# Cross-attention block on one core: VectorE's transposes ahead of a block's second work item, and statistics and norms in other places

## The chip, the cores and the metric

The kernel runs on one core of a Trainium2 chip. The metric is device time in microseconds (us), median of the runs; lower is better. Everything is computed in fp32.

## The reference

A transformer block with cross-attention, for B = 4 batches of L = 512 tokens, D = 512, H = 16 heads of HD = 32, and an inner size of 2048. The mask of the drawn inputs is all ones.

```python
x = layer_norm(hidden_states, ln1_w, ln1_b)                      # (4, 512, 512)
q = (x @ q_w + q_b)                 # -> (B, H, L, HD)
k = (encoder_hidden_states @ k_w + k_b)
v = (encoder_hidden_states @ v_w + v_b)
scores = einsum('bhqd,bhkd->bhqk', q, k) * scale
scores = where(mask, scores, finfo.min)
out = einsum('bhqk,bhkd->bhqd', softmax(scores), v)
hidden = out @ cproj_w + cproj_b + hidden_states
y = layer_norm(hidden, ln2_w, ln2_b)
y = gelu(y @ fc_w + fc_b, approximate=True) @ proj_w + proj_b
return hidden + y
```

## The kernel before

**Tiles.** There are 128 partitions, so a batch has 4 token tiles (NT), and the 16 heads make 4 groups of 4 heads (NG, HG). A window `w` (0 to 15) is one batch with one group of heads. A window has two halves, and a *block* `p` (0 to 31, `w, half = divmod(p, 2)`) is the attention of one half: two query tiles `q0`, `q1`, four heads each, 512 keys.

**A block** (function `block`) does this. `scores` issues eight matmuls (L259), each into a PSUM bank of its own. All dense accumulators, `tp`, `av` and score tiles take PSUM banks in one rotation of eight (`acc_tile`): the n-th tile can be written only when the reader of tile n-8 is done with it. `soften` takes one score tile: VectorE adds the mask `mb` and reduces a minimum (L265), ScalarE takes the exponential with its sum (L269). The results stand in six slots. `turn` transposes a pair of slots in 32x32 squares on VectorE (L277), four times per block, into `tb`. The sums' reciprocal (VectorE, L294) is spread by ScalarE (`rr`, L296) and transposed by VectorE too (L300). `exchange` then calls `copies`, which moves the 32-partition strips of `tb` to their places: four copies on POOL (L329) and twelve DMAs, most of them on SP's queue (L335), into `pT`, `gt` or `xe`, as soon as that target is free. Two blocks later (three in the first blocks) `attend` multiplies with `v` on TensorE (`av`, L352), and VectorE scales `av` into `oT` (L357), which also frees the target and calls `exchange` again.

**Work inside blocks.** Three calls `fill(0)`, `fill(1)`, `fill(2)` in `block` take the other work from a list per block, made with `put(p, ...)`: projections `prep_k`, `prep_q`, `prep_v` (TensorE; ScalarE copies `acck`, `accq`, `accv` out at L219, L230, L244; POOL adds the bias of `v` at L251 or, for window 0, in `v_bias`), the first layer norm of the next batch, the output projection `cproj`, and the MLP's products. `run` takes items until their costs reach a budget: an item has a cost (CHAIN for a dense chain, more for an FC product, 0 for what `do` makes), and an item is still taken if the spent cost and half of its own stay within the budget.

**Layer norm.** `ln_stat` is statistics and aggregate of one token tile on VectorE (L127, L128), `ln_rs` a short chain on POOL (L133 to L140), `ln_norm` normalises one tile on ScalarE (L145) for the keys in `NORM_ACT`, on VectorE (L149) for the others, `ln_turn` transposes on TensorE (`tp`, L158) and applies weight and bias while copying out, on VectorE (L161) or ScalarE (L163). A key is (1 or 2, batch): first or second norm.

**Products of the MLP.** An FC item runs a product on TensorE (L507), ScalarE copies one part `p` out (L510), VectorE adds up (L467), ScalarE takes the gelu (L525). The gelu and the exponential need different tables, which ScalarE loads when they alternate. A projection item (PJ) accumulates `accp` on TensorE (L555), and VectorE adds it to the hidden state (L559).

**Order.** `manual_schedule` means that each engine gets its instructions in the order in which the program writes them. So the order of calls in `block`, the lists given to `put` and the code ahead of the loop fix every engine's queue; the waits between engines come on top. TensorE runs the next block's scores while VectorE and ScalarE finish the block before.

**The start.** Ahead of the loop, the loads go to SP's queue in the order of the program: weights, context and `x` of batch 0, `row`, mask, weights of window 1, then the eight `fc_w` tiles of `load_mlp` (L456). `x` of batch 1 is loaded into the `xn` tiles after that (`load_x`, L176). Its statistics are taken in the fills of blocks 0 and 1, and its four norms, on ScalarE, in block 2.

Of the kernel before, what the change touches and what calls it, by code (L numbers as in the profile page):

```python
# [12 lines left out]
F32 = mybir.dt.float32  # L13
# [7 lines left out]
P = 128  # L21
B, L, D, H = 4, 512, 512, 16
HD = D // H
INNER = 4 * D
NT = L // P
# [7 lines left out]
NW = B * NG  # L33
# [6 lines left out]
NORM_ACT = BY_ACT + ((2, 0), (2, 1))  # L40
# [10 lines left out]
def xattn_block(ctx: ExitStack, tc: tile.TileContext, x, encT, mask, q_w, k_w, v_w, c_w, fc_w, p_w, vecs, rows, out):  # L51
    nc = tc.nc
# [5 lines left out]
    const, keep, hids, tiles, small = pools(ctx, const=1, keep=1, hids=6, tiles=4, small=4)  # L58
# [17 lines left out]
    gt = const.tile([P, NI * (PW + 2 * HD)], F32, tag="gt", name="gt")  # L76
# [36 lines left out]
    S = {}  # L113
# [9 lines left out]
    def ln_stat(key, t, src):  # L123
        if t == 0:
            S["mv", key] = small.tile([P, NT, 2], F32, tag="mv", name=f"mv{key[0]}_{key[1]}")
        st = small.tile([P, 6], F32, tag="st", name=f"st{key[0]}_{key[1]}_{t}")
        nc.vector.bn_stats(st, src)  # L127
        nc.vector.bn_aggr(S["mv", key][:, t, :], st)  # L128
# [12 lines left out]
            S["nm", key] = nm  # L141

    def ln_norm(key, t, dst, src):
        if key in NORM_ACT:
            nc.scalar.activation(  # L145
                dst, src, AF.Identity, bias=S["nm", key][:, t : t + 1], scale=S["rs", key][:, t : t + 1]
            )
            return
        nc.vector.tensor_scalar(  # L149
            dst, src, S["mv", key][:, t, 0:1], S["rs", key][:, t : t + 1], ALU.subtract, ALU.mult  # L150
        )
# [17 lines left out]
    def load_enc(b):  # L169
        for d in range(ND):  # L170
            queue(b).dma_start(out=eT[:, d, :], in_=encT[b, ts(d, P), :])
# [30 lines left out]
    def load_w(w, queue=None, names=("wk", "wq", "wv")):  # L202

        if w >= NW:
            return
        g = w % NG
        for i, (n, src) in enumerate((("wk", k_w), ("wq", q_w), ("wv", v_w))):
            if n in names:
                S[n, w] = kqv_w(w, i)
                (queue or Q[0]).dma_start(out=S[n, w], in_=src[:, g, :, :])  # L210
# [11 lines left out]
    def prep_q(w):  # L222
        b, g = divmod(w, NG)
        qT = k_q(w, 1)
        acc = acc_tile(f"accq_{w}")
        for d in range(ND):
            nc.tensor.matmul(acc, S["wq", w][:, d, :], xT[:, d, :], start=(d == 0), stop=(d == ND - 1))  # L227
        load_w(w + 2, names=("wq",))

        nc.scalar.activation(qT, acc, AF.Identity, bias=qb[:, g : g + 1], scale=-scale)  # L230
        S["qT", w] = qT

    def prep_v(w):
        b = w // NG
        v = five.tile([P, NT, P], F32, tag="v", name=f"v_{w}")
        acc = acc_tile(f"accv_{w}")
        for t in range(NT):
            for d in range(ND):
                nc.tensor.matmul(  # L239
                    acc[:, ts(t, P)], eT[:, d, ts(t, P)], S["wv", w][:, d, :],  # L240
                    start=(d == 0), stop=(d == ND - 1),
                )
        load_w(w + 2, names=("wv",))
        nc.scalar.copy(v, acc.rearrange("p (t f) -> p t f", t=NT))  # L244
        S["v", w] = v
        if w:
            v_bias(w)

    def v_bias(w):
        v, bias = S["v", w], row[:, 2, ts(w % NG, P)]  # L250
        nc.gpsimd.tensor_tensor(v, v, bias[:, None, :].broadcast_to([P, NT, P]), ALU.add)  # L251
# [9 lines left out]
    def soften(w, qt, *heads):  # L261
        for h in heads:
            s = score_tile()
            mn = small.tile([P, 1], F32, tag="mn", bufs=2 * HG, name=f"mn_{w}_{qt}_{h}")
            nc.vector.tensor_tensor_reduce(  # L265
                out=s, in0=S["sc", w, qt][h], in1=S["mb", w // NG], scale=1.0, scalar=FMAX,
                op0=ALU.add, op1=ALU.min, accum_out=mn,
            )
            nc.scalar.activation(s, s, AF.Exp, bias=mn, scale=-1.0, accum_out=S["sums", w][:, qt, h : h + 1])  # L269
            if h % 2:  # L270
                S["ps", w, qt, h // 2] = score_pair()

    def turn(w, qt, k):

        tb = S["tb", w, qt // 2]
        tv = tb[:, :, :PW].rearrange("p j (a t h q) -> p a h t j q", a=2, t=NT, h=HG)
        nc.vector.transpose(tv[:, qt % 2, 2 * k : 2 * k + 2], S["ps", w, qt, k])  # L277

    def block(w, half, fill):

        q0, q1 = 2 * half, 2 * half + 1
        if half == 0:
            S["sums", w] = small.tile([P, NT, HG], F32, tag="sums", name=f"sums_{w}")
        tb = S["tb", w, half] = two.tile([P, NI, PW + 2 * HD], F32, tag="tb", name=f"tb_{w}_{half}")
        scores(w, q0)
        scores(w, q1)
        soften(w, q0, 0, 1, 2, 3)
        soften(w, q1, 0, 1)
        turn(w, q0, 0)
        soften(w, q1, 2, 3)  # L290
        fill(0)
        turn(w, q0, 1)
        rs = small.tile([P, 2, HG], F32, tag="rsum", name=f"rsum_{w}_{half}")
        nc.vector.reciprocal(rs, S["sums", w][:, 2 * half : 2 * half + 2, :])  # L294
        rr = one.tile([P, 2, HG, HD], F32, tag="rr", name=f"rr_{w}_{half}")
        nc.scalar.copy(rr, rs[:, :, :, None].broadcast_to([P, 2, HG, HD]))  # L296
        turn(w, q1, 0)
        fill(1)
        turn(w, q1, 1)
        nc.vector.transpose(  # L300
            tb[:, :, PW:].rearrange("p j (a q) -> p a j q", a=2), rr.rearrange("p a h d -> p (a h d)")
        )
        waiting.append((w, half))
        if w < NW - 1 or half == 0:
            exchange()
        fill(2)

    waiting, held = [], {}
# [5 lines left out]
    def exchange():  # L314

        while waiting and target(*waiting[0]) not in held:
            w, half = waiting.pop(0)
            held[target(w, half)] = w, half
            copies(w, half)
# [513 lines left out]
    CHAIN, TURN = 3.4, 0.5  # L833

    def do(fn):
        return [(0.0, fn)]
# [13 lines left out]
    def turns1(b):  # L850
        return [(TURN, lambda d=d: ln1_turn(b, d)) for d in range(ND)]
# [10 lines left out]
    def inputs(b):  # L862
        ln = [(0.0, lambda part=part: ln1(b, part)) for part in range(3)]
        return do(lambda: load_x(b)), ln, turns1(b), do(lambda: load_enc(b))

    def run(work, budget=None):

        spent = 0.0
        while work and (budget is None or spent + work[0][0] / 2 <= budget):
            cost, fn = work.pop(0)  # L870
            fn()
            spent += cost
        return spent
# [15 lines left out]
    nc.sync.dma_start(out=row, in_=rows[None, :, :].broadcast_to([P, 3, D]))  # L889
    load_mask(0, nc.sync)  # L890
    load_w(1, nc.sync, ("wv", "wq"))

    load_mlp()

# [3 lines left out]
    prep_v(0)  # L898
    prep_k(1)
    run(turns1(0))  # L900
    x1, x2, x3, x4 = inputs(1)
    run(x1)
    load_h(0, *range(NT))
    nc.sync.dma_start(out=wc, in_=c_w)
    make_mb(0)
    nc.vector.tensor_scalar(qb, vec[:, QB : QB + NG], 0.0, -scale, ALU.add, ALU.mult)
    prep_q(0)
    v_bias(0)


    mlp = []
# [3 lines left out]
    def some(n):  # L915
        taken = []
        while n > 0:
            n -= 1 if mlp[0][0] == CHAIN else 2
            taken.append(mlp.pop(0))
        assert n == 0  # L920
        return taken
# [4 lines left out]
    def h_(b, *ts_):  # L926
        return do(lambda: load_h(b, *ts_))
# [7 lines left out]
    def rs(b):  # L935
        return do(lambda: ln_rs((2, b)))

    def stat(b, *ts_):
        return do(lambda: [stat2(b, t) for t in ts_])
# [6 lines left out]
    def put(p, *work, before=()):  # L946

        work = [item for part in work for item in part]
        ahead[p] = list(before)
        fills[p] = work  # L950

    k2, q2, v2 = A(2)
    k3, q3, v3 = A(3)
    k4, q4, v4 = A(4)
    k5, q5, v5 = A(5)
    k6, q6, v6 = A(6)
    put(0, [(CHAIN, lambda: prep_v(1)), v2, k2], x2[:1])
    put(1, [k3, (0.0, lambda: prep_q(1)), (CHAIN, lambda: (prep_v(3), load_enc(1)))], x2[1:2])
    put(2, [q2], x2[2:], [k4])
    put(3, [q3, v4])  # L960
    put(4, x3[:2], [k5], x3[2:])
    put(5, [v5, q4])
# [15 lines left out]
    k, q, v = A(10)  # L978
    put(13, [k], some(2), [v], x2[:1])
    put(14, [q], some(2))  # L980
    put(15, some(2), x2[1:2], some(2))

    k, q, v = A(11)
    put(16, h_(1, 0, 1), x2[2:], [k, q], x3[:2], some(2), x3[2:3])
    put(17, [v], x3[3:], h_(1, 2, 3), x4, cb(1), C(1))
    k, q, v = A(12)
    put(18, [q], some(2), [k])
    put(19, some(2), [v])
    k, q, v = A(13)
    put(20, [k, q], some(2), stat(1, 0, 1))  # L990
    put(21, [v], some(2), stat(1, 2, 3), rs(1))
    k, q, v = A(14)
    t2 = turns2(1)
    put(22, [k, q], norm(1, 0, 1), some(2), norm(1, 2, 3))
# [14 lines left out]
    for p in range(2 * NW):  # L1009
        w, half = divmod(p, 2)  # L1010
        if half == 0 and w and w % NG == 0:
            make_mb(w // NG)
        run(ahead[p])
        for pair in due.get(p, ()):
            attend(*divmod(pair, 2))

        def fill(n, work=fills[p]):
            run(work, CHAIN if n < 2 else None)

        block(w, half, fill)  # L1020
    exchange()

    first_c = FIRST * FQ // 2
    load_h(B - 1, *range(NT))
# [59 lines left out]
```

## Time and profile before

| | before |
| --- | --- |
| median of 3 runs | 777.32 us (776.58 to 777.48) |
| the profiled execution | 776.39 us, of which the span is 774.6 us |
| PE (TensorE matmul) busy | 767.5 us, 99% of the span, 4442 matmuls |
| DVE (VectorE) busy | 622.6 us, 80% |
| ACT (ScalarE) busy | 338.4 us, 44% |
| POOL (GpSimd) busy | 298.7 us, 39% |
| DMA | 119.37 MB, mean 154 GB/s |
| chain that ended last | PE 96%, DVE 2%, DMA 1% |

In the rows, a time stands at the start of a line if it is one of the timeline (us from the start of the span, then duration, engine, line, operation, tiles written and read, and how many instructions of a kind lie together). What stands in brackets is the idle time ahead of the instruction and what ended it. Matmuls are pipelined: a matmul that stands in the queue behind a waiting one, or waits behind a running one, is shown as busy.

### The profile page before, as it was taken

Reading aid. Unit: us, or ns where it says so; the run is one execution under the profiler, and the core shown is the slowest. Engines: PE = TensorE matmul, PEld = TensorE weight load, DVE = VectorE, ACT = ScalarE, POOL = GpSimd, SP = SyncE. Lnnn points to the kernel's source line nnn. Section 1 sums busy time; section 2 is a strip of 40 time slices with the busy share of each in tenths; the row PEclk is TensorE's granted clock in tenths of the full one; section 3 lists DMA queues with packets and bytes.
Section 4 is the critical chain, followed back from the end, with each engine's and each line's share of the span. In section 5 each row is a group of like instructions: output and inputs, shape, how many; then the busy total and the mean of one; then the engine's idle time right before and its main releaser. Section 6 shows DMA issues by size and latency. Waiting matters only on the chain.

```text
span 774.6 us, 12975 instructions
## 1 busy us (share of the span) xinstructions
PE 767.5 (99%) x4442; PEld 519.3 (67%) x4442; DVE 622.6 (80%) x1262; ACT 338.4 (44%) x760; POOL 298.7 (39%) x311
## 2 busy tenths in 40 slices
PE   9999999999999999999999999999999999999998
PEld 6655555467754745565554556446888889988897
DVE  3798999787988857877887889877878999679863
ACT  2577767477774626547663567401201221012200
POOL 1435446377355364224573553350060024300052
PEclk9999999999999999999999999999999999999999
DMA  8978778457766766664656586783523330023001
GB/s 329 309 223 216 183 200 229 125 151 177 224 167 162 183 181 169 156 173 121 162 136 189 144 240 167 207 254 122 199 84 98 90 115 14 28 83 95 1 16 41
DMA packets 54818, 119.37 MB, mean 154 GB/s; under 512 B 10417, under 2 KB 13617, under 8 KB 54625
## 3 DMA queue, kind: packets, MB, share of 16 engines
q1 hardware_dynamic: 53424, 114.88, 53.3%
q0 software_dynamic: 896, 2.82, 1.2%
q10 hardware_dynamic: 432, 0.86, 0.5%
q8 instruction: 35, 0.57, 0.3%
q14 instruction: 31, 0.25, 0.1%
HBM read 58.22 MB, written 6.82 MB: 84 GB/s over the span
## 4 chain that ended last, share of the span: by engine, by line
PE 96%; DVE 2%; DMA 1%; SPq 0%; issue 0%; ACT 0%; ACTq 0%; POOL 0%; DVEq 0%; POOLq 0%
PE q L507 25%; PE accp L555 9%; PE sc L259 8%; PE accv L239 8%; PE acck L217 7%; PE r L645 7%; PE accq L227 7%; PE av L352 7%; PE accc L392 7%; PE q4p L682 2%; PE q1p L700 2%; PE tp L158 2%; PE q2p L682 1%; DMA xe<-tb 1%; DVE tb L277 1%; PE warm L888 1%
## 5 line engine op out<-in xcount | busy, mean ns | idle before, releaser
L269 ACT ACTIVATE ptt<-ptt,mn 128x512 f32<-128x512 f32 x256 | 181.6, 710 | 125.8 <-DVE mn L265 125.8
L265 DVE CUSTOM_DVE_ANT_0 ptt<-sc,mb 128x512 f32<-128x512 f32 x256 | 161.5, 687 | 21.5 <-PE sc L259 16.9
L277 DVE STREAM_TRANSPOSE tb<-ptt 128x1024 f32<-128x1024 f32 x128 | 155.1, 1221 | 0.0
L329 POOL COPY pT<-tb 32x1088 f32<-32x1088 f32 x96 | 104.3, 1087 | 52.8 <-DVE oT L357 32.8
L555 PE MATMUL accp<-pbt,gt 128*128 128x512 f32 x192 | 85.1, 597 | 0.0
L507 PE MATMUL q<-yT,gt 128*128 128x256 f32 x320 | 78.9, 379 | 0.0
L259 PE MATMUL sc<-pbt 32*128 32x512 f32 x512 | 70.7, 616 | 1.5 <-ACT pbt L230 0.8
L555 PEld LDWEIGHTS accp<-pbt,gt 128*128 128x128 f32 x192 | 35.7, 190 | 47.6 <-issue 39.7
L507 PEld LDWEIGHTS q<-yT,gt 128*128 128x128 f32 x320 | 60.8, 190 | 8.7 <-issue 0.5
L525 ACT ACTIVATE ga<-ga,vec 128x512 f32<-128x512 f32 x40 | 26.7, 714 | 87.9 <-DVE ga L467 87.9
L239 PEld LDWEIGHTS accv<-ptt,xe 128*128 128x128 f32 x512 | 59.0, 192 | 8.4 <-DVE mn L265 5.3
L507 PE MATMUL q<-ys,gt 128*128 128x256 f32 x240 | 61.7, 379 | 0.0
L239 PE MATMUL accv<-ptt,xe 128*128 128x128 f32 x512 | 60.2, 276 | 0.0
L217 PE MATMUL acck<-xe,ptt 128*128 128x512 f32 x128 | 58.7, 601 | 0.0
L227 PE MATMUL accq<-xe,ptt 128*128 128x512 f32 x128 | 58.2, 597 | 0.0
L392 PE MATMUL accc<-wc,oT 128*128 128x512 f32 x128 | 56.1, 595 | 0.0
L507 PEld LDWEIGHTS q<-ys,gt 128*128 128x128 f32 x240 | 45.5, 190 | 6.6 <-DVE gt L464 0.4
L259 PEld LDWEIGHTS sc<-pbt 32*128 32x128 f32 x512 | 28.5, 183 | 30.9 <-issue 17.0
L269 ACT ACTIVATION_READ_ACCUMULATOR ptt<-ptt,mn 128x1 f32 x256 | 47.8, 187 | 0.0
L352 PE MATMUL av<-pT,v 128*32 128x256 f32 x768 | 46.4, 382 | 0.0
L217 PEld LDWEIGHTS acck<-xe,ptt 128*128 128x128 f32 x128 | 23.5, 192 | 31.0 <-issue 22.5
L251 POOL TENSOR_TENSOR v<-v,row 128x512 f32<-128x512 f32 x16 | 20.3, 1272 | 61.5 <-ACT v L244 61.5
(179 smaller groups left out, 1187.1 us busy)
## 6 DMA issues: line engine op xcount, KB each, us to landing
pT<-tb SPq DMA_DIRECT2D x288, 136.0 KB, 2.4
pbt<-p_w_dram SPq DMA_DIRECT2D x40, 256.0 KB, 3.1
gt<-fc_w_dram SPq DMA_DIRECT2D x40, 256.0 KB, 2.6
gt<-tb SPq DMA_DIRECT2D x48, 136.0 KB, 2.8
pbt<-fc_w_dram SPq DMA_DIRECT2D x24, 256.0 KB, 3.3
xe<-tb SPq DMA_DIRECT2D x42, 136.0 KB, 2.8
ptt<-k_w_dram SPq DMA_DIRECT2D x16, 256.0 KB, 3.9
xe<-encT_dram SPq DMA_DIRECT2D x16, 256.0 KB, 4.0
```

The costliest lines, as they stand in the source:

```text
L217: nc.tensor.matmul(acc, S["wk", w][:, d, :], eT[:, d, :], start=(d == 0), stop=(d == ND - 1))
L227: nc.tensor.matmul(acc, S["wq", w][:, d, :], xT[:, d, :], start=(d == 0), stop=(d == ND - 1))
L239: nc.tensor.matmul(acc[:, ts(t, P)], eT[:, d, ts(t, P)], S["wv", w][:, d, :], start=(d == 0), stop=(d == ND - 1),)
L259: nc.tensor.matmul(S["sc", w, qt][h], qT[r, ts(qt, P)], kT[r, :], start=True, stop=True)
L265: nc.vector.tensor_tensor_reduce(out=s, in0=S["sc", w, qt][h], in1=S["mb", w // NG], scale=1.0, scalar=FMAX, op0=ALU.add, op1=ALU.min, acc ...
L269: nc.scalar.activation(s, s, AF.Exp, bias=mn, scale=-1.0, accum_out=S["sums", w][:, qt, h : h + 1])
L277: nc.vector.transpose(tv[:, qt % 2, 2 * k : 2 * k + 2], S["ps", w, qt, k])
L329: nc.gpsimd.tensor_copy(pT[ts(i, HD), i], tb[ts(i, HD), i])
L352: nc.tensor.matmul(av[ts(h, HD), : 2 * P].rearrange(shape, **kw), v[:, t, ts(h, HD)], p[t][h], start=(t == 0), stop=(t == NT - 1),)
L392: nc.tensor.matmul(acc, S["oT", b][:, g, ts(t, P)], wc[:, g, :], start=(g == 0), stop=(g == NG - 1))
L507: nc.tensor.matmul(o, x[:, k], y[:, k], start=(k == 0), stop=(k == 1))
L555: nc.tensor.matmul(acc, gT[q % 2][:, k, ts(t, P)], S["pw", b, q * FQ + k], start=(k == 0), stop=(k == FQ - 1))
```

## The change

The change has six parts.

1. In `block`, VectorE's second `turn` of `q0` goes ahead of `fill(0)`, and the last `turn` and the transpose of `rr` go ahead of `fill(1)`; the reciprocal now stands behind the first `turn` of `q1`. `exchange` stays behind `fill(1)`. In the last block it is now called there as well, and no longer behind the loop.
2. `fill(0)` does nothing where the block's first item costs more than CHAIN. Of the lists given, that is block 29, which starts with an FC product: it now has its two products in `fill(1)` and `fill(2)`.
3. `x` of batch 1 is loaded into `gt` ahead of `load_mlp`, its statistics and `ln_rs` stand ahead of the first `prep_q`, and its four norms (`norm1`, ScalarE, from `gt` into the `xn` tiles) in the last fill of block 0.
4. The last two of the key (2, 0)'s four norms (block 10) go from ScalarE to VectorE.
5. The four norms of batch 3 (VectorE) go from block 16 into block 15, between the last two PJ items.
6. The four statistics of key (2, 1) and its `ln_rs`, which stood at the end of blocks 20 and 21, go into block 20 ahead of its PJ items.

TensorE's instructions keep their order, one for one.

```diff
     def ln_norm(key, t, dst, src):
-        if key in NORM_ACT:
+        if key in NORM_ACT and (key != (2, 0) or t < 2):
...
         soften(w, q1, 0, 1)
         turn(w, q0, 0)
         soften(w, q1, 2, 3)
+        turn(w, q0, 1)
         fill(0)
-        turn(w, q0, 1)
+        turn(w, q1, 0)
         rs = small.tile([P, 2, HG], F32, tag="rsum", name=f"rsum_{w}_{half}")
         nc.vector.reciprocal(rs, S["sums", w][:, 2 * half : 2 * half + 2, :])
         rr = one.tile([P, 2, HG, HD], F32, tag="rr", name=f"rr_{w}_{half}")
         nc.scalar.copy(rr, rs[:, :, :, None].broadcast_to([P, 2, HG, HD]))
-        turn(w, q1, 0)
-        fill(1)
         turn(w, q1, 1)
         nc.vector.transpose(
             tb[:, :, PW:].rearrange("p j (a q) -> p a j q", a=2), rr.rearrange("p a h d -> p (a h d)")
         )
         waiting.append((w, half))
-        if w < NW - 1 or half == 0:
-            exchange()
+        fill(1)
+        exchange()
         fill(2)
...
     load_w(1, nc.sync, ("wv", "wq"))
+    for t in range(NT):
+        nc.sync.dma_start(out=gt[:, ts(t, D)], in_=x[1, ts(t, P), :])
     load_mlp()
...
     run(turns1(0))
-    x1, x2, x3, x4 = inputs(1)
-    run(x1)
     load_h(0, *range(NT))
     nc.sync.dma_start(out=wc, in_=c_w)
     make_mb(0)
     nc.vector.tensor_scalar(qb, vec[:, QB : QB + NG], 0.0, -scale, ALU.add, ALU.mult)
+    for t in range(NT):
+        ln_stat((1, 1), t, gt[:, ts(t, D)])
+    ln_rs((1, 1))
     prep_q(0)
     v_bias(0)
+
+    def norm1(b, *ts_):
+        for t in ts_:
+            S["xn", b][t] = tiles.tile([P, D], F32, tag="xn", name=f"xn1_{b}_{t}")
+            ln_norm((1, b), t, S["xn", b][t], gt[:, ts(t, D)])
+
+    S["xn", 1] = [None] * NT
+    x3 = turns1(1)
...
-    put(0, [(CHAIN, lambda: prep_v(1)), v2, k2], x2[:1])
-    put(1, [k3, (0.0, lambda: prep_q(1)), (CHAIN, lambda: (prep_v(3), load_enc(1)))], x2[1:2])
-    put(2, [q2], x2[2:], [k4])
+    put(0, [(CHAIN, lambda: prep_v(1)), v2, k2], do(lambda: norm1(1, *range(NT))))
+    put(1, [k3, (0.0, lambda: prep_q(1)), (CHAIN, lambda: (prep_v(3), load_enc(1)))])
+    put(2, [q2], [k4])
...
-    put(15, some(2), x2[1:2], some(2))
+    put(15, some(2), x2[1:2], some(1), x2[2:], some(1))
...
-    put(16, h_(1, 0, 1), x2[2:], [k, q], x3[:2], some(2), x3[2:3])
+    put(16, h_(1, 0, 1), [k, q], x3[:2], some(2), x3[2:3])
...
-    put(20, [k, q], some(2), stat(1, 0, 1))
-    put(21, [v], some(2), stat(1, 2, 3), rs(1))
+    put(20, [k, q], stat(1, 0, 1, 2, 3), rs(1), some(2))
+    put(21, [v], some(2))
...
         def fill(n, work=fills[p]):
-            run(work, CHAIN if n < 2 else None)
+            if n or not work or work[0][0] <= CHAIN:
+                run(work, CHAIN if n < 2 else None)
 
         block(w, half, fill)
-    exchange()
```

## The prediction

> **What bounds the kernel now.** I read the page first, then PE's waits, then the chain that ended last in order of time, and last the timelines around each place where the chain runs slow.
>
> ```profile
> PE 767.5 (99%) x4442; PEld 519.3 (67%) x4442; DVE 622.6 (80%) x1262; ACT 338.4 (44%) x760; POOL 298.7 (39%) x311
> ```
>
> ```profile
> PE av L352 <- DMA xe<-tb: 0.9, 1, 0.9
> ```
>
> TensorE is busy throughout and carries the chain, and the order of instructions shows that the change leaves its stream as it is, matmul for matmul. So the time moves only by what TensorE waits. Its own waits look tiny (the longest but the start's is 0.9 us, above), but a matmul that waits behind a running one counts as busy. The eight score tiles of a block are the same work each time, so their group shows the hidden waits:
>
> ```profile
> 47.38 1.93 PE sc L259 x16
> ...
> 58.24 3.19 PE sc L259 x16
> ...
> 80.00 3.62 PE sc L259 x16
> ```
>
> 1.93 us is the undisturbed group. Block 3 (58.24) pays 1.26 on top, block 5 (80.00) 1.69; blocks 21 and 22 follow below. The last score tiles of a group need PSUM banks that the block before used last: its dense accumulators and `av`. What frees them late is a VectorE or ScalarE queue that runs late. These places, and the 0.9 us before the last `attend`, are all that can be won.
>
> **Statistics and norms of batch 1.** In block 2 ScalarE runs four norms ahead of the `rr` copy:
>
> ```profile
> 55.99 2.32 DVE L277 STREAM_TRANSPOSE tb<-ptt 128x1024 f32<-128x1024 f32 x2
> 56.26 2.92 ACT L145 ACTIVATE xn<-xn,nm,rs 128x512 f32<-128x512 f32 x4
> 59.08 0.39 ACT L296 COPY rr<-rsum 128x256 f32<-128x256 f32 x1
> 59.50 0.45 DVE L300 STREAM_TRANSPOSE tb<-rr 128x256 f32<-128x256 f32 x1 [1.19 <-ACT rr L296]
> ```
>
> The norms hold `rr` to 59.08, so VectorE stands still for 1.19 us, and the `acck` copy behind `rr` and the `oT` product behind the `rr` transpose free their banks only after 59.9, inside block 3's group. The change moves the norms to block 0. Then, with the reciprocal now behind one more transpose (2.32 for two, 1.16 each), `rr` runs at 57.2, `acck` leaves at 58.2, the `rr` transpose at 58.3, `oT` at 58.9. The second half of the group is due at 58.17 + 0.97 = 59.1: nothing is late next. **Gain 1.26.** In block 0 the four norms (2.92) stand behind the last `acck` copy, and block 1's exponentials queue behind them by about 1.7 us. VectorE's four statistics leave blocks 0 and 1 (3.2 us), which pays for that: I get the end of VectorE's block 1 at 46.4, before the next scores at 47.4.
>
> The statistics go to the start, ahead of the first softmax:
>
> ```profile
> 10.61 5.88 SPq L456 DMA_DIRECT2D pbt<-fc_w_dram  x8
> 23.20 0.69 DVE L265 CUSTOM_DVE_ANT_0 ptt<-sc,mb 128x512 f32<-128x512 f32 x1 [4.27 <-PE sc L259]
> ```
>
> A statistic with its aggregate takes at most 0.88 (334.80 to 335.97 less 0.29, below); four are 3.5 us, in a hole of 4.27. Their four loads go to SP ahead of the eight `fc_w` loads, so they get those loads' first places, issued from 10.61 on at about 0.7 us each. At the 6 us from issue to landing that loads of this stretch show (`xn` loads: 5.8 to 6.0) the last lands near 19, and its statistic is due at 22.3. Moved back by 2.7 us are the eight loads, which block 11 needs first, and the next `wk` and `wv`, which TensorE needs at 31.4 and 27.6; they stood at issue 16.9 to 18.2, so some 2 us are left. On POOL four small operations pass the `v` biases, which block 3 needs first. Cost 0.
>
> **Statistics inside block 20, VectorE's order in block 21.**
>
> ```profile
> 335.20 2.37 PE sc L259 x15
> ```
>
> ```profile
> 334.80 0.66 DVE L127 BATCH_NORM_STATS2 st<-h 128x6 f32<-128x512 f32 x1
> ...
> 335.97 0.42 DVE L357 TENSOR_TENSOR oT<-av,pT 128x256 f32<-128x256 f32 x1 [0.29 <-DMA pbt<-p_w_dram]
> ```
>
> Block 20's two statistics end just before `oT` and hold it, and block 21's group pays 0.44. All four now run right behind the softmax, where VectorE idles. **Gain 0.44**; the `rs` chain on POOL passes the exchange's copies, which wait for the next `oT` anyway.
>
> ```profile
> 349.19 0.40 DVE L300 STREAM_TRANSPOSE tb<-rr 128x256 f32<-128x256 f32 x1
> 349.51 0.65 DVE L127 BATCH_NORM_STATS2 st<-h 128x6 f32<-128x512 f32 x1
> ```
>
> ```profile
> 349.18 1.99 PE L259 MATMUL sc<-pbt 32*128 32x512 f32 x14
> 351.94 1.12 PE L259 MATMUL sc<-pbt 32*128 32x512 f32 x2 [0.77 <-DVE oT L357]
> ```
>
> In block 21 the product's four adds, a transpose, the `rr` transpose and two statistics stand ahead of `oT`, and the last score tile waits for it to 351.94. Block 22's group runs from 349.18 to 353.06 (351.94 + 1.12): 3.88 for 1.93. Now the transposes come before the adds, and the statistics are gone. In whatever order, the work that is left is done where the first statistic began, 349.51; `oT` (0.42) then ends by 349.95, before the second half of the group is due at 350.2. **Gain 1.88.**
>
> **Two norms of batch 0 to VectorE, block 10.**
>
> ```profile
> 160.80 1.27 POOL L251 TENSOR_TENSOR v<-v,row 128x512 f32<-128x512 f32 x1 [3.56 <-ACT v L244]
> 161.75 0.41 DVE L300 STREAM_TRANSPOSE tb<-rr 128x256 f32<-128x256 f32 x1
> 163.30 1.91 PE L158 MATMUL tp<-ident,xn 128*128 128x128 f32 x16
> 253.33 1.91 DVE L149 TENSOR_SCALAR xn<-xn,mv,rs 128x512 f32<-128x512 f32 x4
> 515.54 5.34 POOL L363 TENSOR_TENSOR pbt<-pbt,row 128x512 f32<-128x512 f32 x4 [0.88 <-DMA pbt<-x_dram]
> 517.55 2.21 DVE L149 TENSOR_SCALAR h<-h,mv,rs 128x512 f32<-128x512 f32 x2
> ```
>
> With POOL idle a norm takes 0.48 (four in 1.91); beside POOL's adds two took 2.21. The two norms start at 162.1 and TensorE transposes their rows from 163.5 on. With `rr` 1.1 later on ScalarE, the `v` copy and so POOL's bias add slide from 160.8 to about 161.8, so the add runs until 163.1 and the weight sums follow. At 0.48 each nothing is late; at 1.1 each, and a second norm behind another sum, the last row is ready at 163.1 to 164.9 against 163.6. I take the nearer row, POOL busy, one POOL operation waited for by each: 164.3. **Cost 0.65**, bounds 0 and 1.3. The Trainium skill ("SBUF — State Buffer", on engine and DMA ports) says that the port pair shared by VectorE and GpSimd is an exclusive lock held for a whole instruction; it speaks against this edit, and by it I would price 0.65 too, without it 0. The trace agrees at 517.55.
>
> **Four norms of batch 3, block 15.** They go on VectorE ahead of the last product's add:
>
> ```profile
> 244.13 0.69 DVE L559 TENSOR_TENSOR h<-accp,h 128x512 f32<-128x512 f32 x1 [1.28 <-PE accp L555]
> 244.74 0.42 DVE L197 TENSOR_SCALAR mb<-m 128x512 f32<-128x512 uint8 x1
> 246.44 0.42 DVE L357 TENSOR_TENSOR oT<-av,pT 128x256 f32<-128x256 f32 x1 [1.27 <-issue]
> ```
>
> VectorE waits there for 1.28 + 1.27 = 2.55 us, and four norms at 0.48 are 1.9. **Cost 0**; if that cover were gone (1.1 each), 4.4 - 2.55 = 1.9, but POOL has nothing to do in this stretch that would make it so.
>
> **The transposes ahead of the second item; blocks 28, 29, 30.** Where the second item is a product (12, 13, 14, 18, 21, 28) its adds slide by 1.16 + 0.33 = 1.49. In 12, 14 and 28 VectorE has no gap there, so the sum and `oT` stay; the gelus behind the adds slide, and the next exponentials with them. Block 29 also loses its first fill: both products now follow the softmax.
>
> ```profile
> 477.63 2.93 PE L259 MATMUL sc<-pbt 32*128 32x512 f32 x16
> ```
>
> ```profile
> 460.62 1.34 ACT L525 ACTIVATE gt<-gt,vec 128x512 f32<-128x512 f32 x2 [1.76 <-DVE gt L467]
> 461.97 1.28 ACT L269 ACT_TABLE_LOAD   x1
> 463.27 0.72 ACT L269 ACTIVATE ptt<-ptt,mn 128x512 f32<-128x512 f32 x1
> ```
>
> ```profile
> 469.88 0.69 DVE L467 TENSOR_TENSOR gt<-q,p 128x512 f32<-128x512 f32 x1 [1.23 <-ACT p L510]
> ...
> 474.89 0.65 DVE L467 TENSOR_TENSOR gt<-q,p 128x512 f32<-128x512 f32 x1
> 475.65 1.95 DVE L467 TENSOR_TENSOR gt<-q,gt 128x512 f32<-128x512 f32 x3
> ...
> 479.00 0.38 DVE L357 TENSOR_TENSOR oT<-av,pT 128x256 f32<-128x256 f32 x1
> ```
>
> The exponentials of block 29 start at 464.8, not 463.27, and hold the first transpose by some 0.3. VectorE was free for more at 468.65 (469.88 less the 1.23 that it waited for `p`); so from 468.9 it now does three transposes, the reciprocal and `rr` (3.9) to 472.8, and the first product's adds (2.71, as 474.89 to 475.65 + 1.95) to 475.5. Its gelus (1.34) end at 476.9. Only then does ScalarE copy `p` of the second product (0.36 on the same engine), to 477.2; the adds end at 479.9 and `oT` starts at 479.8 instead of 479.00. Block 30's group, which takes 2.93 by that `oT`, pays this in full. **Cost 0.77**; bounds 0 and 1.49 (all of the slide). The Trainium skill ("ScalarE: Activation LUTs", What ACT_TABLE_LOAD costs) gives about 2.66 us for a switch of tables, a drain included; here the next exponential starts 1.30 after the load does. At 2.66 block 30 would lose about 1.4 more.
>
> **The exchange in block 31** has nothing but the third item behind it, whose only work is on TensorE and VectorE. But the `accp` add ahead of its transposes goes behind them:
>
> ```profile
> 503.24 0.65 DVE L559 TENSOR_TENSOR h<-accp,h 128x512 f32<-128x512 f32 x1
> ```
>
> They end some 0.6 earlier, so the last landing is too, and the 0.9 us wait shrinks. **Gain 0.6**, bounds 0 and 0.94. Block 5's 1.69 stays, set by ScalarE's copies of `tp`, which the change leaves where they are:
>
> ```profile
> 80.99 1.45 ACT L163 ACTIVATE xe<-tp,vec 128x512 f32<-128x512 f32 x2
> ```
>
> **Sum.** 1.26 + 0.44 + 1.88 + 0.6 = 4.2; less 0.65 + 0.77 = 1.4: 2.8 us gained. The profiled execution took 776.39 us (774.6 of it the span), which becomes 773.6; it lies 0.9 under the median of the runs, 777.32, which becomes 774.6, some 0.35% less.
>
> **Rivals.** *The gain is taken back at block 5.* If VectorE bounds blocks 3 to 8, the 1.26 returns as a longer wait at block 5, and the time is 775.8. For it: transposes and softmax fill some 10.4 of a block's 11 us. Against it:
>
> ```profile
> 71.58 0.69 DVE L265 CUSTOM_DVE_ANT_0 ptt<-sc,mb 128x512 f32<-128x512 f32 x1 [0.59 <-PE sc L259]
> ```
>
> it waited for TensorE in block 4. Chance 0.12.
>
> *Slower: ScalarE becomes the bound behind the gelus.* Blocks 13, 15 and 29 start their exponentials 1.49 late, block 30 2.3. If all of it reached TensorE, 6.8 less the 0.77 counted: 774.6 + 6.0 = 780.6. It decides where the lateness is more than ScalarE's slack in the block: eight exponentials are 5.7 of 11 to 14 us, which speaks against it; for it speaks that VectorE had no gap there either. Half of it is enough to reach 777.6. Chance 0.11.
>
> *A drain at each switch*, as that page has it, costs about 1.4 in block 30: 776.0. Chance 0.03, since no load in this trace shows one.
>
> **Numbers.** The forecast has 0.74; a measurement of this kernel tells about 0.2% (1.55 us) from no change. Of the 0.74 some 0.05 ends under that gain, with the unknown costs at their bad ends. Faster 0.69, same 0.20 (with the first and third rival), slower 0.11. The range reaches from all unknown costs at 0 and the last wait gone (gain 4.5: 772.8) past the first rival with the bad ends of blocks 10 and 29 (0.65 + 0.72): 777.2.
>
> **Right or wrong.** The score groups of blocks 3, 21 and 22 should read 1.93, that of block 5 still 3.6, that of block 30 about 3.6, and the last `av` should wait 0.3. The transposes of block 10 show a wait for VectorE of 0.65 if the lock holds. I am wrong if block 1's or 2's group grows (loads or norms too late), or if groups 13 to 15 grow over 1.93 (gelus).

## The result, and the profile after

The changed kernel is slower: median 778.69 us (776.62 to 781.21, 13 runs) against 777.07 us (776.27 to 777.48, 13 runs), a ratio of 1.0027 with an interval of 1.0015 to 1.0039. The prediction had 774.6 and faster. Its runs also spread over 4.6 us, those of the kernel before over 1.2.

TensorE's order is the same in both kernels, so each matmul of one profiled execution can be laid beside the same matmul of the other. The difference of their start times changes only at a few places. Between them it stays within a few tenths:

| place | predicted | measured, us |
| --- | --- | --- |
| before any changed instruction, and the first chains | 0 | +0.94 |
| block 3's score group | -1.26 | -1.18 |
| block 10's transposes of `tp` | +0.65 (with the next row) | +0.64 |
| block 11's score group | | +0.38 |
| block 21's score group | -0.44 | -0.44 |
| block 22, ahead of `av` | 0 | +0.30 |
| block 22's score group | -1.88 | -1.89 |
| block 30's score group | +0.77 | +0.75 |
| last `av` | -0.6 | +1.97 |
| the last MLP's `r` | 0 | +0.27 |
| sum | -2.8 | +1.74 |

The sum agrees with the page (span 776.3 against 774.6, profiled execution 778.31 against 776.39). The first +0.94 is no effect of the change: a context load that is issued at the same time in both, ahead of everything that changed, landed at 7.07 us instead of 5.35. The kernel before was lucky there in the execution that was profiled: in the four other profiles of kernels with its start (e2, e9, e10, e11 below) TensorE's first chains end 0.3 to 0.7 later than in it. Nor did the forecast have a row for the 0.30 ahead of block 22's `av` and the 0.27 in the last MLP; no run gives a cause for them.

In the waits of PE in the changed kernel (waited for, us in total, times, longest), the first line is new in size; it read 0.9 before:

```profile
PE av L351 <- DMA xe<-tb: 2.9, 1, 2.9
PE warm L887 <- POOL nhalf L878: 1.4, 1, 1.4
PE sc L259 <- ACT pbt L230: 0.8, 1, 0.8
PE tp L158 <- DVE xn L149: 0.5, 1, 0.5
PE av L351 <- DVE gt L466: 0.2, 1, 0.2
```

The chain of waits in order of time (start, duration) gives the score groups of blocks 3, 5, 22 and 30 in the changed kernel, answering to 3.19, 3.62, 3.88 and 2.86 (2.93 in the timeline's row) in the kernel before:

```profile
59.26 1.93 PE sc L259 x16
...
79.75 3.62 PE sc L259 x16
...
349.89 1.93 PE sc L259 x16
...
476.45 3.62 PE sc L259 x16
```

Blocks 3 and 22 are at their undisturbed 1.93, block 5 is as it was, block 30 pays what was forecast. The rows of the forecast for blocks 3, 21, 22 and 30 hold; blocks 10 and 11 cost more than the 0.65, within its bounds. The last exchange does not hold. First block 31's weight loads on SP's queue and ScalarE's half of the exchange in the kernel before, then both and SP's half in the changed one, and a row of SP's waits there:

```profile
498.87 1.87 SPq L456 DMA_DIRECT2D pbt<-p_w_dram  x4
505.44 3.16 ACTq L335 DMA_DIRECT2D xe<-tb  x5
```

```profile
499.39 8.88 SPq L455 DMA_DIRECT2D pbt<-p_w_dram  x4
504.36 4.18 ACTq L334 DMA_DIRECT2D xe<-tb  x6
508.37 3.92 SPq L334 DMA_DIRECT2D xe<-tb  x6
```

```profile
SPq L455 <- DMA xe<-tb: 7.7, 4, 7.0
```

The four `p_w` loads of block 31's first projection, which took SP 1.87 us at 498.87 in the kernel before, are spread over 8.88 us: SP issues one, and then stands for 7.0 us until a DMA `xe<-tb` has landed. That is one of the exchange's six DMAs on ScalarE's queue, which can go out only when `tb` is complete (504.36; landed at 506.71). So three loads of 256 KB go out at 506.78 to 507.88, in the middle of the exchange, and SP's six DMAs of the exchange stand behind them. The last one lands at 516.45, where it landed at 514.87 before.

Why a weight load waits for another queue's copy is seen in the built program, and the traces name the same semaphores (a semaphore is a counter on which an engine waits). DMAs of SP and ScalarE are counted on eight semaphores, handed out in turn over both queues together, and a DMA first waits until the one before it on its semaphore has landed. The start shows it too: the second load of `k_w` leaves at 5.47 in the kernel before and at 7.08 in the changed one, just behind the landing of the context load with the same semaphore (5.35 and 7.07). The turn follows an order that is merged from all engines. With the transposes ahead of `fill(1)`, ScalarE's exchange DMAs get earlier places in it. In the kernel before, all four loads got semaphores last used by the exchange of block 30, whose copies landed at 498.81 to 500.20, each just ahead of its load. In the changed one, the second and third load got those of ScalarE's first two copies of block 31, and the fourth stands behind them in SP's queue.

### The profile page after: what moved, and what is told of

Its sections match the earlier page's. It is cut to its first block, busy times and chain, and to the rows that moved or that the text cites. A ratio compares the mean times of both kernels' runs of the same rounds, so it can differ in the third digit from the quotient of the medians.

```text
span 776.3 us, 12971 instructions
## 1 busy us (share of the span) xinstructions
PE 767.1 (99%) x4442; PEld 519.9 (67%) x4442; DVE 625.2 (81%) x1264; ACT 337.2 (43%) x758; POOL 299.4 (39%) x311
## 4 chain that ended last, share of the span: by engine, by line
PE 88%; DVE 8%; DMA 1%; issue 1%; SPq 0%; ACT 0%; POOL 0%; DVEq 0%; ACTq 0%; POOLq 0%
PE q L506 20%; PE accp L554 10%; PE sc L259 8%; PE av L351 7%; PE r L644 7%; PE accc L391 7%; PE acck L217 7%; PE accq L227 7%; PE accv L239 7%; PE q4p L681 2%; DVE ga L466 2%; PE tp L158 2%; PE q1p L699 1%; DVE ptt L265 1%; DVE tb L277 1%; DVE gs L463 1%
## 5 line engine op out<-in xcount | busy, mean ns | idle before, releaser
L259 PE MATMUL sc<-pbt 32*128 32x512 f32 x512 | 69.0, 616 | 0.8 <-ACT pbt L230 0.8
```

What stands on the lines that cost most here:

```text
L259: nc.tensor.matmul(S["sc", w, qt][h], qT[r, ts(qt, P)], kT[r, :], start=True, stop=True)
```

## The experiments

The theory under test: the 2 us lost at the last exchange, and what follows from TensorE's longer pause there, turn a gain into a loss. Medians are compared with runs of the kernel before on the same chip.

**e1: block 31 alone in the old order, in the changed kernel.**

```diff
+        if w == NW - 1 and half == 1:
+            (the lines of the kernel before, fill(1) ahead of the last turn)
+        else:
+            (the lines of the changed kernel)
...
         block(w, half, fill)
+    exchange()
```

> The changed kernel, but block 31 alone in the order of the kernel before (its transposes, and the exchange behind the loop). Theory A: what was lost is lost in the last exchange. There the eight semaphores on which DMAs are counted are handed out in turn; three of SP's four p_w loads of block 31 got semaphores behind ScalarE's exchange DMAs, waited 7 us for the first of those to land, and went out among the exchange's own DMAs. Here they get semaphores behind the exchange before it and go out by 501: the wait ahead of the last av falls from 2.91 to 0.9 (0.6 to 1.2), the median from 778.7 to 776.5 (776.0 to 777.0), and the spread of the runs falls from 4.6 us to under 2. Rival B: the loss lies elsewhere (the loads of x at the start, the clock), the wait there is only its last place: the median stays at 778 or above, with the spread.

776.19 us (775.32 to 776.89) against 776.35 before: ratio 0.9995 (0.9986 to 1.0004). SP issues the four loads from 498.81 to 500.41, the last exchange DMA lands at 514.97, and the wait is 1.4, above the 0.9 (0.6 to 1.2) that was expected:

```profile
PE av L370 <- DMA xe<-tb: 1.4, 1, 1.4
```

2.5 us of the changed kernel's time and its spread are gone with one block's order. What is left equals the kernel before, not the forecast's gain.

**e2: block 31 alone in the new order, in the kernel before.** The mirror image, with the same switch on the other kernel.

> The kernel before, with block 31 alone in the new order. By the semaphores that it gets, two p_w loads (the third and fourth) wait for ScalarE's first exchange DMA here, not three. Theory A: they go out among the exchange, the wait ahead of the last av rises from 0.94 to about 2.2 (1.7 to 2.6), the median from 777.1 to 778.3 (777.8 to 778.8). Rival B: transposes that end 0.6 earlier shorten the wait to about 0.3, median 776.5; or nothing changes, 777.1.

779.39 us (778.94 to 780.18), ratio 1.0038 (1.0026 to 1.0051): one block's order, with nothing else changed, makes the kernel slower by as much as the whole change does, or more (the intervals overlap). Two loads went out late (507.71 and 508.13), the last exchange DMA landed at 516.75, and TensorE's wait is 2.42 where 2.2 was expected. The median is above the expected 778.8, and the windows of PE behind the wait (stretch, us, PE busy, granted clock, DMA share, GB/s) show what was added in the profiled execution:

```profile
516.00:518.00 2.00, 0.90 (x18) 1.00 1.03 365
518.00:520.00 2.00, 2.00 (x21) 0.60 1.06 391
520.00:522.00 2.00, 2.00 (x3) 0.55 1.04 384
522.00:524.00 2.00, 2.00 (x6) 1.00 0.95 344
```

```profile
518.40:521.82 3.42, 3.42 (x15) 0.50 1.05 385
```

The clock falls to a half from 518.40 to 521.82, behind the pause (514.68 to 517.10). Matmul by matmul, that costs 1.65 us more. Three of the five runs had a mean clock of 0.997 or 0.998 (779.39 to 780.18 us), the other two 1.000, and these lie at 778.94 and 779.01: lower, but above 778.8 as well, so the clock is not all that was added.

**e3: the four loads on GpSimd's queue,** in the changed kernel. In the trace its loads are counted on semaphores of their own (111 and 116 to 118, where SP and ScalarE have 100 to 107).

```diff
+        Q[0] = nc.gpsimd if p == 2 * NW - 1 else nc.sync
         block(w, half, fill)
+        Q[0] = nc.sync
```

> The changed kernel, with the four p_w loads of block 31 on GpSimd's DMA queue, which stands idle there and counts on semaphores of its own. SP's first exchange DMA then waits for no landing of ScalarE's. Theory A: both halves of the exchange start together, at about 504.4, the last one lands by 511 to 512, before TensorE comes for it at 513.8: the wait ahead of the last av falls from 2.91 to 0 to 0.3, the median from 778.7 to 775.8 (775.2 to 776.3), 1.3 under the kernel before. Rival B: 778 or above.

775.03 us (774.1 to 776.95), ratio 0.9982 (0.9973 to 0.9991). The wait ahead of the last `av` is 0.40, put down to GpSimd. The gain on the kernel before, 1.3, is as expected, one reason isn't: the last exchange DMA lands at 513.66, not by 512. From first issue to last landing the exchange takes 9.4 us in the kernel before, 9.5 here, 9.9 in e1, 11.5 with two loads among it (e2) and 12.1 with three. So what counts is that no load goes out among it; that both halves start together makes it no shorter here.

**e4: a longer pause,** in the changed kernel.

```diff
-                q.dma_start(out=pT[ts(j, HD), i], in_=tb[ts(i, HD), j])
+                cuts = (0, 544, 1088) if w == NW - 1 and half else (0, 1088)
+                for c0, c1 in zip(cuts, cuts[1:]):
+                    q.dma_start(out=pT[ts(j, HD), i, c0:c1], in_=tb[ts(i, HD), j, c0:c1])
```

> The changed kernel, with each DMA of the last exchange cut into two (24 of half the size instead of 12). Issues of 0.6 us each, six more on each queue: TensorE's wait ahead of the last av grows by about 3.6, from 2.9 to some 6.5 us. Theory C on the spread of the changed kernel's runs (776.6 to 781.2, granted clock 0.995 to 1.000): a TensorE pause of about 3 us sometimes lets the granted clock fall behind it. Then here the clock falls in every run, the windows behind the wait show it, and the time grows by more than the added wait: 784 to 788. Rival: pause and clock have nothing to do with each other: 782.3, clock as before, and the spread unchanged.

784.14 us (782.95 to 784.58), ratio 1.0097 (1.0083 to 1.011), as theory C has it. The waits and the windows:

```profile
PE av L353 <- DMA xe<-tb: 6.9, 1, 6.9
```

```profile
516.00:518.00 2.00, 0.00 (x0) 0.64 0.49 113
518.00:520.00 2.00, 1.11 (x9) 0.50 0.67 180
520.00:522.00 2.00, 2.00 (x27) 0.50 0.90 290
522.00:524.00 2.00, 2.00 (x13) 0.66 1.01 358
524.00:526.00 2.00, 2.00 (x6) 1.00 0.98 360
```

```profile
516.55:523.38 6.83, 4.49 (x33) 0.50 0.77 234
```

All four runs had a mean granted clock of 0.993 to 0.996. The `av` behind the pause takes 4.12 us instead of 1.93. So pause and clock belong together. For the changed kernel's spread that is shown by the runs' mean clocks, not by a profile of a slower run: in the changed kernel, whose pause is 2.91, six of 13 runs had a mean clock of 0.995 to 0.998, at 779.74 to 781.21 us; the other seven (0.999 or 1.000) lie at 776.62 to 778.69, with a mean of 777.9. In the 63 runs of the kernel before that stood beside these experiments, and in the 81 of the kernels whose last wait is 1.4 or less, it was never under 0.999.

**e5: the moves of statistics and norms alone,** on the kernel before: parts 3, 5 and 6 of the change, in the diff above, without parts 1, 2 and 4.

> The kernel before, with only the moves of statistics and norms (batch 1 to the start and block 0, batch 3's norms to block 15, key (2, 1)'s statistics into block 20); transposes, block 29, block 10 and the last exchange as before. Theory A (the gains of the prediction belong to the moves alone, the costs to the transposes' new places, block 10's norms and block 29): the score groups of blocks 3, 21 and 22 go to 1.93 to 2.0, the p_w loads of block 31 wait for nothing, the last av waits 0.9 as before: 1.2 + 0.4 + 1.9 = 3.5 us under the kernel before, some 772.9 against 776.4 (772.3 to 773.8). Rival B (the transposes ahead of the second item are needed for block 22, where the product's adds stand ahead of oT): block 22 keeps 1.9 of its wait, 774.8.

774.13 us (773.91 to 774.92) against 776.98: ratio 0.9963 (0.995 to 0.9975), 2.9 us less. The chain shows the groups of blocks 3, 21 and 22:

```profile
49.78 7.24 DMA xe<-encT_dram
57.02 0.04 issue
57.07 1.13 PE acck L217 x2
58.19 1.86 PE av L352 x32
60.06 1.93 PE sc L259 x16
```

```profile
335.52 1.93 PE sc L259 x16
...
349.13 1.93 PE sc L259 x16
```

All three are undisturbed, in the old order of the transposes. Block 16's score group and the transposes behind it gained another 0.24, which nobody had expected; it is likely that this comes from batch 3's norms, which block 16's VectorE no longer has. The 3.5 forecast wasn't reached. In the execution that was profiled, TensorE waited for the next batch's context (first row), as it did in some of the profiles of other kernels too, and that of e2, with the start of the kernel before, among them.

**e6: the moves, with the loads on GpSimd's queue.**

> As the kernel with the moves alone, and the four p_w loads of block 31 on GpSimd's DMA queue. By its semaphores SP's first exchange DMAs wait for no landing of ScalarE's, so both halves start together and the last lands about 2.4 us earlier: the wait ahead of the last av (0.94) goes. Theory A: 0.9 us under the kernel with the moves alone, 4.4 under the kernel before: 772.0 (771.4 to 772.8). Rival: the four loads' places change nothing else and the wait was covered by POOL or the statistics: the same time as with the moves alone.

773.74 us (772.43 to 773.99), ratio 0.9952 (0.994 to 0.9965). The last `av` waits for nothing, but the forecast of 772.0 wasn't reached: it lies 0.4 under the moves alone, which the intervals don't tell apart from nothing. The 0.9 has moved to the `av` before, block 30's, which waited for nothing with the moves alone:

```profile
503.31 1.93 PE L352 MATMUL av<-pT,v 128*32 128x256 f32 x32 [0.87 <-DMA pT<-tb]
```

On GpSimd's queue the four loads no longer stand behind SP's copies of block 30's exchange. They go out at 494.04 to 495.87, among these copies, and the last copy lands at 503.06 instead of 498.73. So here the loads leave one exchange and fall into the one before it. It is still the lowest ratio of all kernels.

**e7: block 29's product back in its first fill,** in the changed kernel with the loads on GpSimd's queue.

```diff
-            if n or not work or work[0][0] <= CHAIN:
-                run(work, CHAIN if n < 2 else None)
+            run(work, CHAIN if n < 2 else None)
```

> The changed kernel with p_w loads of block 31 on GpSimd's queue, and block 29's first product back in its first fill. Theory A: block 30's score group, 3.7 in the changed kernel, goes back to about 2.9 or less: 0.75 under the changed kernel with GpSimd's loads (775.0 against 776.35 before), so 774.3 (773.8 to 774.9). Rival: the transposes' new place alone makes oT late in block 29 (adds 1.49 later), the group stays at 3.4 or more, 775.0.

773.68 us (773.03 to 774.73) against 776.98, ratio 0.9959 (0.9945 to 0.9972), where the same kernel with the skip had 0.9982. Block 30's group goes from 3.62 to

```profile
475.80 2.62 PE sc L259 x16
```

**e8: all four norms of block 10 on ScalarE,** in the same kernel with the skip.

```diff
-        if key in NORM_ACT and (key != (2, 0) or t < 2):
+        if key in NORM_ACT:
```

> The changed kernel with p_w loads of block 31 on GpSimd's queue, and all four norms of key (2, 0) back on ScalarE. Theory A (VectorE's and GpSimd's shared port: the norms take 1.07 instead of 0.48 and push the sums behind them): TensorE's wait of 0.64 in block 10's transposes goes, and block 11's score group falls from 2.48 to 2.1: 1.0 less, 774.0. Rival B (the rr copy, now 0.7 later on ScalarE, holds its four norms until 164.2, with the fourth row needed at 163.6): a wait of about 0.6 stays at the transposes, only block 11's 0.4 goes: 774.6.

775.34 us (774.43 to 776.37), ratio 0.9976 (0.9967 to 0.9985). Rival B holds in the trace: matmul by matmul the transposes lose 0.9 (0.64 in the changed kernel), now to ScalarE, and block 11's group is back at 2.08. The ratio, 0.9976 for 0.9982, doesn't tell the two kernels apart.

```profile
163.61 1.64 PE L158 MATMUL tp<-ident,xn 128*128 128x128 f32 x13 [0.38 <-ACT xn L145]
```

**e9: only the loads on GpSimd's queue, in the kernel before.**

> The kernel before, with nothing but the four p_w loads of block 31 on GpSimd's DMA queue. SP's first exchange DMA then stands behind no landing of ScalarE's. Theory A: the wait of 0.94 ahead of the last av goes, 0.9 us under the kernel before (0.5 to 1.2). Rival: the exchange's halves were not held by each other, no change.

776.84 us against 776.73, ratio 1.0 (0.9991 to 1.0009): a miss. In the trace the last wait fell from 0.94 to 0.48, half of what was expected; the exchange took 9.0 us instead of 9.4. A gain of that size does not show in the medians. The loads landed at 505.05 instead of 504.38.

**e10: the new order of the transposes alone,** with the loads on GpSimd's queue so that the last exchange says nothing: part 1 of the change on the kernel before.

> As the kernel before with p_w loads of block 31 on GpSimd's queue, and VectorE's transposes in the changed kernel's order in every block (no statistics or norms moved, block 29 and block 10 as before). Theory A: the order alone only costs: 0.7 at block 10's transposes (the rr copy and so the norms 0.7 later on ScalarE), 0.3 at block 22's av; blocks 3, 21 and 22 keep their waits of 1.26, 0.44 and 1.9. So 1.0 us over the kernel with GpSimd's loads alone (0.6 to 1.5). Rival B: the order makes part of the gain at block 22 (transposes done ahead of the product's adds), up to 1.3 of it, and the sum is 0 or below.

778.19 us (777.17 to 779.13) against 776.73, ratio 1.002 (1.0011 to 1.0029); 1.35 above the kernel with these loads alone. Rival B's sum falls, but a part of it is there: block 22's group gains 0.47. Beside block 10's transposes (0.9) there is a second place of cost, which nobody had expected: batch 3's norms, still in block 16, now stand behind one more transpose on VectorE, and TensorE's `tp` loses 1.27 us to them.

```profile
255.01 1.24 DVE L277 STREAM_TRANSPOSE tb<-ptt 128x1024 f32<-128x1024 f32 x1
256.18 1.88 DVE L149 TENSOR_SCALAR xn<-xn,mv,rs 128x512 f32<-128x512 f32 x4
```

So the order needs the move of these norms to block 15, but the move doesn't need the order. The 0.3 ahead of block 22's `av` is in the traces of kernels with the old order as well (0.3 in e9, 0.5 in e11), so I don't put it down to the order.

**e11: two norms of block 10 on VectorE alone,** in the old order, with the loads on GpSimd's queue: part 4 of the change on the kernel before.

> As the kernel before with p_w loads of block 31 on GpSimd's queue, and only the last two norms of key (2, 0) on VectorE (old order of the transposes). Theory A (two norms beside GpSimd's adds take 2.1, not 0.96): they run from 162.1 to 164.2, TensorE waits 0.5 to 0.7 for the fourth row at 163.6, and block 11's group pays 0.4 for the sums behind them: 1.0 us over the kernel with GpSimd's loads alone. Rival B: with rr in its old place GpSimd's bias add is over sooner, the norms fall among its short sums, take about 1.5, and cost 0.3 or less.

777.0 us (776.38 to 777.59), ratio 1.0001 (0.9992 to 1.001), against 776.84 for the loads alone. Rival B is nearer. The norms take 1.92 for two, beside GpSimd's add:

```profile
161.14 1.92 DVE L149 TENSOR_SCALAR xn<-h,mv,rs 128x512 f32<-128x512 f32 x2
```

The first, begun ahead of GpSimd's add, takes 0.50, the second 1.49. But they start at 161.14, ahead of the last transpose, and end in time: no wait at `tp`, and block 11's group 0.17 longer than in the kernel before.

## Why the prediction was wrong

**The step that failed** is the last exchange: "has nothing but the third item behind it, whose only work is on TensorE and VectorE", gain 0.6. It looked at what stands behind the call of `exchange` and at the transposes' earlier end, and not at what stands ahead of the exchange in SP's queue. The transposes do end earlier: ScalarE's first exchange DMA leaves at 504.36 instead of 505.44, which is 0.6 earlier counted from TensorE's matmuls, as forecast. But the `p_w` loads of the first item, ahead of the call in both kernels, now wait for that DMA to land, go out among the exchange, and lose more than the 0.6. The call's new place ahead of the third item was not tested alone. Measured: +1.97 in the trace where -0.6 stood, 2.57 of the 4.5 us between forecast and trace, shown by e1 and e2 from both sides. The rest of the trace's 4.5 is the 0.94 at the start, which is no effect of the change, 0.37 in blocks 10 and 11, and the 0.30 and 0.27 whose cause is open.

**What no part of the prediction had** is the clock behind the pause: 1.65 us in e2's profile, and a lowered mean clock in six of the changed kernel's 13 runs. Those runs lie at 780.4 on average, 2.6 above the others. No rival named a lower clock.

**Blocks 3, 21 and 22** were right in place and size (-1.18, -0.44, -1.89), and e5 shows that they belong to the moves. For block 22 the prediction gave "the transposes come before the adds, and the statistics are gone" as one reason; the statistics alone do it (e5). The order alone brings 0.47 there (e10).

**Block 10** came to 1.02 where 0.65 was taken, within the bounds of 0 and 1.3. The mechanism is the forecast one: the norms run from 161.84 to 163.97, `tp` waits for VectorE and loses 0.64; the 0.38 in block 11's group, behind the same norms, was not forecast.

```profile
161.84 2.13 DVE L149 TENSOR_SCALAR xn<-h,mv,rs 128x512 f32<-128x512 f32 x2
164.02 1.64 PE L158 MATMUL tp<-ident,xn 128*128 128x128 f32 x13 [0.47 <-DVE xn L149]
```

Two norms beside GpSimd's adds take 2.13, close to the 2.21 of the quoted row, so the shared port of the Trainium skill ("SBUF — State Buffer") agrees with the trace. But the cost was put down to the wrong edit. On VectorE in the old order the norms cost 0.17 (e11), and in the new order `tp` loses 0.9 with all four norms on ScalarE (e8, e10), since the `rr` copy runs 1.0 later there, counted from TensorE's matmuls (1.1 was taken), behind one more transpose. So the new order costs about 1 us with the norms on either engine; the prediction used the later `rr` for GpSimd's adds only.

**Blocks 29 and 30** were right in the sum (+0.75 for 0.77); e7 shows that skipping the fill is the cause, since the transposes' new place alone leaves the group at 2.62. The step on the way holds too. Block 29's exponentials were to start at 464.8 instead of 463.27, 1.5 later. They start at 463.48, but block 29's score group starts 1.24 earlier in the changed kernel (459.78 instead of 461.02); counted from that group they are 1.45 later:

```profile
462.18 1.28 ACT L269 ACT_TABLE_LOAD   x1
463.48 0.72 ACT L269 ACTIVATE ptt<-ptt,mn 128x512 f32<-128x512 f32 x1
```

These rows also answer the third rival: 1.30 from the load's start to the next exponential, as before, with no drain. **Block 15** was right at cost 0, and the 0.24 gained around block 16 in the old order was missed.

**The rivals.** The gain was not taken back at block 5 (3.62 in both). The slower rival, ScalarE behind the gelus, has no row in the trace: the groups of blocks 13 to 15 did not grow. The side it named, slower, came true by another mechanism.

The sum of the parts, as far as the runs show it: moves -2.9 (e5); the new order +1.35 alone (e10), less the 1.27 that the move to block 15 takes back, and without its 0.47 at block 22, which the moves bring already, so +0.55; two norms on VectorE +0.2 (e11); block 29's skip +0.75 (trace); the last exchange about +2.5 with the clock (ratio 1.0027, against 0.9995 in e1). That makes +1.1 against a measured 1.2 to 3.0 (the interval of the ratio, times 777). The rest is of the size of the intervals of the parts. Kernels e5, e6 and e7 beat both: 0.9963, 0.9952 and 0.9959 of the kernel before. That e6 and e7 differ can't be told from these runs.

## What to carry to other kernels

Where DMA completions share a few semaphores in turn, a queue is not independent of the others: moving work on VectorE changed which semaphore a weight load gets, and the load then waited for another queue's copy. Ask of every load near an exchange which earlier DMA it waits for, and put loads that must not wait on a queue with semaphores of its own, or issue them well ahead. Then look where they go out now: in e6 they fell into the exchange before. And when a change bundles moves that fill gaps with a new order of a queue, price the two apart: here the moves bring the gain without the new order.

## What the runs showed of the hardware

A pause of TensorE can cost more than its length. Behind 2.42 us without a matmul the granted clock was 0.50 for 3.42 us, from 518.40 to 521.82 (e2); with a pause of 6.89 us it was 0.50 for 6.83 us, twice as long, from 516.55, still inside the pause, to 523.38 (e4). A pause of 2.91 left it at 1.00 in one profile of the changed kernel, while the mean clock of six of its 13 runs was down, as it was in three of e2's five; so at these lengths it falls in some executions only. The Trainium skill ("TensorE: Matmul & The Clock Gate", Part 1) says that the clock goes to half after an idle window of about 3.4 us that runs free of the kernel, and comes back after as long a busy one. The half, the length of the slow stretch and the run-to-run change agree with these traces. That a window must be idle throughout does not: the 3.42 us ahead of e2's drop hold 2.12 us of the pause and 1.30 us of matmuls, and the trace decides.

A VectorE norm of 128x512 in fp32 takes 0.48 us with GpSimd quiet (four in 1.91). Of e11's two, the one that runs beside GpSimd's add takes 1.49.
